# Second part of an attention and expert kernel: tiles at other addresses, a weight sum made by an adding load, operands stored in one piece

## The chip, the cores and the metric

The kernel runs on one core of a Trainium2 chip, in fp32. The metric is the device time of one execution in microseconds. The time of a version is the median of its runs.

## The reference

Four sequences of 1024 tokens with 1024 features are normalised. A linear attention with a running sum gives `s`. A feed-forward network with eight experts that share one pair of weights, where each expert takes at most 256 tokens, gives `g`. The result is `x + s * g`.

```python
q = jnp.einsum('bld,ed->ble', x, Wq) + bq          # x is the normalised input
k = jnp.einsum('bld,ed->ble', x, Wk) + bk
v = jnp.einsum('bld,ed->ble', x, Wv) + bv
phi_q, phi_k = jax.nn.elu(q) + 1.0, jax.nn.elu(k) + 1.0
kv_sum = jnp.cumsum(phi_k * v, axis=1)
context = (phi_q * kv_sum).reshape(B, L, D) * SCALE
s = jnp.einsum('bld,ed->ble', context, Wo) + bo
...
h = jax.nn.gelu(buf @ w1.T + b1, approximate=False) @ w2.T + b2   # F = 4096
gathered = jnp.where(keep[:, None], h[...], 0.0) * probs_flat[:, None]
out = jnp.zeros_like(x).at[token_idx].add(gathered)
...
return x + s * jax.nn.silu(out)
```

Only tokens that an expert keeps have a `g` that is not zero. So at most 2048 tokens need the network, the queries and the output product.

## The kernel before

**First part (to about 453 us).** It normalises the tokens, makes keys and values with their running sum for the first 2304 tokens, stores these sums in DRAM (`kvs`) and picks the 2048 tokens. Its tiles lie in pools that are closed at its end. The second part's pools take the same addresses, and a tile of the second part waits until the tile that lay there is done with.

**Second part.** The chosen tokens are worked on in two passes (`p`) of 1024. A pass has five stages of 14 products: four pairs `hidden` and `ffn_out`, one for each quarter of the 4096 hidden features, and then the pair `queries` and `result`. Each pair member multiplies two matrices of 1024 x 1024 with Strassen's scheme: each matrix is cut into quarters, and 7 products of quarters or of their sums take the place of 8. A product is 48 matmuls: each fp32 operand is split into a high part in fp32r (`cast`, on ScalarE) and a remainder (`low`, on VectorE), and three of the four combinations are multiplied. There are 140 products, numbered by a step `n`; `n0` is the step before a member's first product.

The work around the products is written out by hand. `on(n, phase, f)` hangs a piece on a step. At each step the program emits the matmuls and then the pieces of ten phases:

```python
PHASES = ("load", "pre", "cast0", "evac", "low0", "add", "cast1", "low1", "post", "raw")
```

The instructions of TensorE, VectorE, ScalarE and SP (SyncE, which issues loads and stores) keep this order. [...] 

The pieces that matter here:

- `left_weights` loads the four quarters of a left weight matrix (`left_quarter`, SP, 1 MB each, L766) into five tiles `raw` of 8 KB a partition that `right_weights` uses in turn (L1055), and makes the sums on VectorE (`sub` at L930, `plus` at L933). At step `n0 + 1`, phase `pre`, a sum and a difference are made that product `n0 + 2` needs.
- `fetched` loads the tokens' operands of the next product (1 MB for each half, L976) from DRAM tensors `xtd`, in which the seven operands of a pass lie in split form. Those of the first pass are stored from the tiles that the products use (`keep`, L1100). Those of the second are made by `xprep_items` during steps 14 to 20 and 28 to 34: gather four times (L647), transpose (L240), add, split (L166, L167), store from a tile `o` (L679).
- `Unit` is a tile with one half of a product's operand; `a` and `b` have three each, used in turn, two in the pool `fu`, the third in `fp`.
- `queries` gathers the key sums of its tokens (`fetch`, 16 gathers `gk` on POOL for each quarter), transposes them (`turn`), and multiplies them into the evacuated quarter (`then`, L1228 and L1233).
- `result` adds its four quarters to the output by scatters that add (`done`, L1292, on POOL).
- `small` gives tiles of 4 KB a partition from a pool `sp` of nine. It serves gathers, transposed sums, exponentials, `o`, and also the rows of the biases `b2` and `bo`. `ps` is one of two PSUM tiles of four banks; a product group begins when one of them is evacuated.

Of the kernel before, what the change touches and what calls it, by code (L numbers as in the profile page):

```python
# [18 lines left out]
P = 128  # L19
# [27 lines left out]
def tile_first_tokens(  # L47
# [44 lines left out]
    xtd = [dp.tile([7 * 2 * P, 4 * BT], F32, name=f"xtd_{p}") for p in range(NP)]  # L92
# [562 lines left out]
    def xprep_items(p, buf):  # L655
# [3 lines left out]
        def item(j):  # L659
# [13 lines left out]
            def out_of(i, src):  # L673
                o = buf(f"o{p}_{j}_{i}")
                oh = o.bitcast(F32R).rearrange("p (u h k t) -> h p u k t", u=2, h=2, k=2)
                split((oh[0], oh[1]), src.rearrange("p (u k t) -> p u k t", u=2, k=2))
                dst = xtd[p].rearrange("(i u p) (s t) -> i u p s t", i=7, u=2, s=4)[i - 1]
                for u, ou in enumerate(o.rearrange("p (u s t) -> u p s t", u=2, s=4)):
                    nc.gpsimd.dma_start(dst[u, :, :, j * P : (j + 1) * P], ou)  # L679

            def plain():
                out_of(1, v[0, 0])
                out_of(2, v[1, 0])

            def sums():
                t = buf(f"t{p}_{j}")
# [5 lines left out]
            def sums2():  # L692
                nc.vector.tensor_tensor(v[0, 1], v[1, 1], v[0, 1], ALU.subtract)
                nc.vector.tensor_tensor(v[1, 0], v[1, 0], v["t2"], ALU.subtract)
                out_of(7, v[0, 1])
                out_of(5, v["t1"])

            def rest():
                out_of(4, v[1, 0])
                out_of(3, v[1, 1])  # L700

            return fetch, turn, plain, sums, sums2, rest
# [61 lines left out]
    def left_quarter(dst, src, i, j):  # L764

        nc.sync.dma_start(  # L766
            dst.rearrange("p m (k f) -> p m k f", k=4),
            src[4 * i : 4 * i + 4, :, 4 * j : 4 * j + 4].rearrange("m p k f -> p m k f"),
        )
# [9 lines left out]
    class Unit:  # L779


        def __init__(self, side, i):

            pool = later["fu" if (i + 1) % 3 < 2 else "fp"]
            self.t = pool.tile(
                [P, 2, 2 * BT], F32R, tag=f"{side}{(i + 1) % 3}", name=name(side)
            )
# [96 lines left out]
    store_sums(queue=nc.gpsimd)  # L884
# [11 lines left out]
    sp = ctx.enter_context(tc.tile_pool(name="sp", bufs=9, reuse_waits="tile"))  # L896

    sp.tile([P, 2 * P], F32, tag="room", bufs=1, name="room")
    fp = ctx.enter_context(tc.tile_pool(name="fp", bufs=1, reuse_waits="tile"))
    later["fp"] = fp  # L900
    fps = ctx.enter_context(tc.tile_pool(name="fps", bufs=2, space=PSUM, reuse_waits="tile"))
# [15 lines left out]
    raw += [quarter(f"raw_{i}") for i in range(2, 5)]  # L917
# [6 lines left out]
    yq[0] = quarter("y0")  # L924
# [56 lines left out]
    def tokens(p, i):  # L981
        return xtd[p].rearrange("(i u p) f -> i u p f", i=7, u=2)[i - 1]
# [43 lines left out]
    def left_weights(n0, src, view=None):  # L1026

        q = dict(zip(((0, 0), (1, 0), (1, 1), "t", (0, 1)), raw))
        raw[:] = (q[k] for k in ((0, 0), "t", (1, 0), (1, 1), (0, 1)))
# [8 lines left out]
        on(max(n0 - 2, -1), "raw", lambda: load((1, 1)))  # L1038
        on(n0 - 1, "raw", lambda: load((0, 1)))

        on(n0, "add", lambda: sub(q["t"], q[0, 0], q[1, 0]))
        on(n0 + 1, "pre", lambda: plus(q[1, 0], q[1, 0], q[1, 1]))
        on(n0 + 1, "pre", lambda: sub(q[0, 0], q[1, 0], q[0, 0]))
        on(n0 + 3, "add", lambda: sub(q[0, 1], q[0, 1], q[0, 0]))
        for k, key in enumerate(((0, 0), (0, 0), (0, 1), "t", (1, 0), (1, 1), (0, 1))):
# [113 lines left out]
    def ffn_out(n0, h, s, y):  # L1159
# [18 lines left out]
        if s == 0:  # L1178

            def row():  # L1180
                y["b"] = small("b2")
# [9 lines left out]
    def queries(n0, p):  # L1191
# [48 lines left out]
        for k, d, key in (  # L1240
            (-14, 2, (0, 0)), (-12, 2, (1, 1)), (-6, 3, (1, 0)), (1, 2, (0, 1))
# [23 lines left out]
    def result(n0, h, y, p):  # L1265
# [4 lines left out]
        def row():  # L1270
            c["b"] = small("bo")
# [62 lines left out]
    for p in range(NP):  # L1334
        y = dict(yq)
        if p + 1 < NP:
            prep = xprep_items(p + 1, small)
            for j, (s, at) in enumerate(
                ((s, at) for s in (1, 2) for at in ((0, 2, 2, 2, 3, 4), (2, 4, 4, 5, 5, 6)))
            ):  # L1340
# [97 lines left out]
```

## Time and profile before

| | |
|---|---|
| median of 3 runs | 2067.14 us (2067.07 to 2069.58) |
| the profiled execution | 2073.87 us, span 2072.1 us |
| TensorE busy | 1978.2 us, 95% |
| VectorE busy | 1508.6 us, 73% |
| ScalarE busy | 756.9 us, 37% |
| POOL busy | 421.7 us, 20% |
| moved by DMA | 360.32 MB, 174 GB/s on average |
| idle time of TensorE before the second part's matmuls | 52.6 us |

A row of a timeline gives start, duration, engine, line, operation, what is written from what, shape and count; in brackets stands the idle time of the engine before it and what ended it. Like instructions that follow each other closely are merged. `PE` is TensorE, `DVE` VectorE, `ACT` ScalarE; a `q` behind a name means the engine's queue. In a row of windows each engine's busy time and count of instructions follow the stretch, then TensorE's clock and the DMA engines' share and GB/s.

### The profile page before, as it was taken

What the parts mean: (1) busy time and instruction counts of PE and PEld (TensorE: products, weight loads), DVE (VectorE), ACT (ScalarE), POOL (GpSimd) and SP (SyncE); (2) the same over time, 40 slices, a digit from 0 to 9 for tenths busy, and PEclk for the clock granted to TensorE, in tenths of its full rate; (3) what the DMA queues carried; (4) which work ended last, traced back from release to release, by engine and by line L of the source; (5) the groups of instructions that cost most, each with busy time, mean ns of one, the idle gap of its engine ahead of it and who ended that gap; (6) DMA issues with size and microseconds to landing.
All of it is one profiled execution on the core that took longest, in us unless ns stands there. A gap on an engine that the chain in (4) does not pass through costs nothing.

```text
span 2072.1 us, 22267 instructions
## 1 busy us (share of the span) xinstructions
PE 1978.2 (95%) x8840; PEld 1631.3 (79%) x8840; DVE 1508.6 (73%) x1376; ACT 756.9 (37%) x874; POOL 421.7 (20%) x387
## 2 busy tenths in 40 slices
PE   7999999989999999999999889899999999999875
PEld 6877878877887887888887677788888888888764
DVE  7868876577876876975887785585685685787884
ACT  2323332225533433532423453342432432343451
POOL 1001104652003502843020068001000001120013
PEclk9999999999999999999999989999999999999988
DMA  8867849638248448447146148515515416426314
GB/s 305 242 195 234 264 124 193 190 80 347 74 147 327 156 146 328 146 163 279 54 162 256 51 103 257 209 62 197 199 61 219 167 61 248 158 82 253 133 21 63
DMA packets 114290, 360.32 MB, mean 174 GB/s; under 512 B 13216, under 2 KB 37792, under 8 KB 96032
## 3 DMA queue, kind: packets, MB, share of 16 engines
q1 hardware_dynamic: 77504, 299.98, 41.1%
q0 software_dynamic: 18240, 42.56, 7.7%
q10 hardware_dynamic: 18432, 16.26, 3.5%
q8 instruction: 72, 1.18, 0.2%
q14 instruction: 42, 0.34, 0.0%
HBM read 292.66 MB, written 73.42 MB: 177 GB/s over the span
## 4 chain that ended last, share of the span: by engine, by line
PE 79%; DVE 6%; issue 6%; POOL 3%; DMA 3%; ACT 2%; ACTq 0%; SPq 0%; DVEq 0%; POOLq 0%
PE ps L1005 61%; PE pk L160 3%; PE pk L161 3%; PE pk L162 3%; PE pv L162 3%; PE pv L160 3%; PE pv L161 3%; POOL gk L647 2%; DMA b<-xtd 2%; POOL out L1292 1%; PE pl L325 1%; DVE hid L1228 1%; DVE hid L933 1%; DVE hid L1233 1%; DMA kvs<-kr 0%
## 5 line engine op out<-in xcount | busy, mean ns | idle before, releaser
L1005 PE MATMUL ps<-b,a 128*128 128x512 f32 x6720 | 1544.5, 392 | 52.6 <-DVE y L933 19.2
L1005 PEld LDWEIGHTS ps<-b,a 128*128 128x128 f32 x6720 | 1271.3, 189 | 325.5 <-issue 26.1
L793 ACT CAST a<-raw 128x1024 fp32r<-128x1024 f32 x140 | 147.2, 1052 | 456.8 <-PE ps L1005 366.4
L647 POOL DMA_INDIRECT gk<-kvs,eighth x128 | 174.0, 1360 | 668.4 <-DVE kv L240 504.8
L796 DVE TENSOR_TENSOR a<-raw,a 128x1024 fp32r<-128x1024 f32 x140 | 170.6, 1221 | 182.7 <-ACT a L793 178.1
L793 ACT CAST a<-hid 128x1024 fp32r<-128x1024 f32 x120 | 126.1, 1051 | 368.9 <-PE ps L1005 261.1
L796 DVE TENSOR_TENSOR a<-hid,a 128x1024 fp32r<-128x1024 f32 x120 | 146.4, 1220 | 64.8 <-ACT a L793 64.6
L796 DVE TENSOR_TENSOR b<-raw,b 128x1024 fp32r<-128x1024 f32 x140 | 170.8, 1220 | 1.6 <-ACT b L793 1.6
L933 DVE TENSOR_TENSOR hid<-ps,hid 128x2048 f32<-128x2048 f32 x52 | 119.0, 2288 | 63.7 <-PE ps L1005 48.7
L930 DVE TENSOR_TENSOR raw<-raw,raw 128x2048 f32<-128x2048 f32 x70 | 160.3, 2290 | 1.1
L793 ACT CAST b<-raw 128x1024 fp32r<-128x1024 f32 x140 | 146.7, 1048 | 1.8 <-DMA xtd<-b 1.8
L933 DVE TENSOR_TENSOR work<-ps,work 128x2048 f32<-128x2048 f32 x40 | 91.5, 2288 | 48.8 <-PE ps L1005 48.8
L160 PE MATMUL pk<-xt,ws_w 128*128 128x512 f32 (+1 forms) x264 | 103.1, 391 | 2.6 <-issue 1.4
L161 PE MATMUL pk<-xt,ws_w 128*128 128x512 f32 (+1 forms) x264 | 102.9, 390 | 2.5 <-issue 1.3
L162 PE MATMUL pv<-xt,ws_w 128*128 128x512 f32 (+1 forms) x264 | 101.3, 384 | 1.3 <-DVE ws_w L167 1.2
L162 PE MATMUL pk<-xt,ws_w 128*128 128x512 f32 (+1 forms) x264 | 102.6, 388 | 0.0
L160 PE MATMUL pv<-xt,ws_w 128*128 128x512 f32 (+1 forms) x264 | 101.6, 385 | 0.0
L161 PE MATMUL pv<-xt,ws_w 128*128 128x512 f32 (+1 forms) x264 | 101.2, 383 | 0.0
L679 POOL DMA_DIRECT2D xtd<-o x56 | 41.4, 876 | 277.9 <-DVE o L167 277.2
L166 ACT CAST ws_w<-wr_w 128x1024 fp32r<-128x1024 f32 x64 | 66.1, 1048 | 82.7 <-issue 39.7
L167 DVE TENSOR_TENSOR ws_w<-wr_w,ws_w 128x1024 fp32r<-128x1024 f32 x64 | 77.8, 1215 | 14.7 <-ACT ws_w L166 11.2
L361 ACT ACTIVATE kb<-pk,bs 128x512 f32<-128x512 f32 (+1 forms) x40 | 25.8, 646 | 134.1 <-PE pk L162 97.2
(183 smaller groups left out, 1653.3 us busy)
## 6 DMA issues: line engine op xcount, KB each, us to landing
b<-xtd SPq DMA_DIRECT2D x126, 1024.0 KB
raw<-in_w SPq DMA_DIRECT2D x64, 1024.0 KB
wr_w<-in_wk SPq DMA_DIRECT2D x32, 512.0 KB
wr_w<-in_wv SPq DMA_DIRECT2D x32, 512.0 KB
xtd<-b SPq DMA_DIRECT2D x14, 1024.0 KB
xtd<-o POOLq DMA_DIRECT2D x56, 256.0 KB
kvs<-kr ACTq DMA_DIRECT2D x32, 256.0 KB
raw<-in_wq SPq DMA_DIRECT2D x8, 1024.0 KB
```

The lines of the kernel that those rows point to most:

```text
L160: nc.tensor.matmul(ps, ws[:, 0, k], mv[:, 0, k, c0:c1], start=k == 0, stop=False)
L161: nc.tensor.matmul(ps, ws[:, 0, k], mv[:, 1, k, c0:c1], start=False, stop=False)
L162: nc.tensor.matmul(ps, ws[:, 1, k], mv[:, 0, k, c0:c1], start=False, stop=k == DC - 1)
L166: nc.scalar.copy(dst[0], src)
L167: nc.vector.tensor_tensor(dst[1], src, dst[0].bitcast(F32), ALU.subtract)
L647: nc.gpsimd.indirect_dma_start(out=dst, out_offset=None, in_=src, in_offset=bass.IndirectOffsetOnAxis(ap=idx, axis=0),)
L679: nc.gpsimd.dma_start(dst[u, :, :, j * P : (j + 1) * P], ou)
L793: nc.scalar.copy(self.parts[0], src)
L796: nc.vector.tensor_tensor(self.parts[1], self.src, self.parts[0].bitcast(F32), ALU.subtract)
L930: nc.vector.tensor_tensor(dst, a, b, ALU.subtract)
L933: nc.vector.tensor_tensor(dst, a, b, ALU.add)
L1005: nc.tensor.matmul(ps[:, m], a(h, k, m), b(l, k), start=s["first"] and u == 0 and k == 0 and i == 0, stop=u == 1 and k == 1 and i == 2, sk ...
```

## The change

1. The tensor `xtd` gets one row of 4096 numbers for each operand and partition, so that an operand piece `o` is stored by one DMA of 512 KB instead of two of 256 KB. The stages of `xprep_items` are cut finer and spread over the steps in another way.
2. One sum of two weight quarters, `q["t"]`, is made by loading one quarter and then loading the second onto it with an adding DMA on POOL's queue, at step `n0 - 1`. The second of these quarters is loaded once more by itself, at step `n0`. The sum on VectorE goes, and the difference is made in place.
3. The pool `fp` is laid out first, in the order room, row, the third units of `a` and `b`, `y0`, `raw_4`, `raw_2`, `raw_3`; `sp` comes behind it, with eight tiles instead of nine. The bias rows and the sums `t` of `xprep_items` use the tile `row`.
4. The last stores of `kvs` are issued from ScalarE's queue instead of POOL's.
5. The last `turn` of `queries` comes three steps after its `fetch` instead of two.

```diff
--- before.py
+++ after.py
@@ -89,7 +89,7 @@
     lst = dp.tile([nt, 2], I32, name="lst")


-    xtd = [dp.tile([7 * 2 * P, 4 * BT], F32, name=f"xtd_{p}") for p in range(NP)]
+    xtd = [dp.tile([7 * P, 2 * 4 * BT], F32, name=f"xtd_{p}") for p in range(NP)]


     ident = kp.tile([P, P], F32, name="ident")
@@ -674,32 +674,33 @@
                 o = buf(f"o{p}_{j}_{i}")
                 oh = o.bitcast(F32R).rearrange("p (u h k t) -> h p u k t", u=2, h=2, k=2)
                 split((oh[0], oh[1]), src.rearrange("p (u k t) -> p u k t", u=2, k=2))
-                dst = xtd[p].rearrange("(i u p) (s t) -> i u p s t", i=7, u=2, s=4)[i - 1]
-                for u, ou in enumerate(o.rearrange("p (u s t) -> u p s t", u=2, s=4)):
-                    nc.gpsimd.dma_start(dst[u, :, :, j * P : (j + 1) * P], ou)
-
-            def plain():
-                out_of(1, v[0, 0])
-                out_of(2, v[1, 0])
+                dst = xtd[p].rearrange("(i p) (s t) -> i p s t", i=7, s=8)[i - 1]
+                nc.gpsimd.dma_start(
+                    dst[:, :, j * P : (j + 1) * P], o.rearrange("p (s t) -> p s t", s=8)
+                )
+
+            def plain(i):
+                out_of(i, v[i - 1, 0])

             def sums():
-                t = buf(f"t{p}_{j}")
+                t = one(f"t{p}_{j}")
                 v["t1"], v["t2"] = t[:, :BT], t[:, BT:]
                 nc.vector.tensor_tensor(v["t1"], v[0, 1], v[0, 0], ALU.subtract)
                 nc.vector.tensor_tensor(v["t2"], v[1, 1], v["t1"], ALU.subtract)
                 out_of(6, v["t2"])

-            def sums2():
+            def sum7():
                 nc.vector.tensor_tensor(v[0, 1], v[1, 1], v[0, 1], ALU.subtract)
+                out_of(7, v[0, 1])
+
+            def sum4():
                 nc.vector.tensor_tensor(v[1, 0], v[1, 0], v["t2"], ALU.subtract)
-                out_of(7, v[0, 1])
-                out_of(5, v["t1"])
-
-            def rest():
                 out_of(4, v[1, 0])
-                out_of(3, v[1, 1])
-
-            return fetch, turn, plain, sums, sums2, rest
+
+            return (
+                fetch, turn, lambda: plain(1), lambda: plain(2), sums, sum7,
+                lambda: out_of(5, v["t1"]), sum4, lambda: out_of(3, v[1, 1]),
+            )

         return [item(j) for j in range(NJ)]

@@ -761,11 +762,12 @@
         nc.vector.tensor_tensor(work[:, 2], work[:, 3], work[:, 2], ALU.subtract)
         nc.vector.tensor_tensor(ht, work[:, 2], work[:, 0], ALU.add)

-    def left_quarter(dst, src, i, j):
-
-        nc.sync.dma_start(
+    def left_quarter(dst, src, i, j, queue=nc.sync, **how):
+
+        queue.dma_start(
             dst.rearrange("p m (k f) -> p m k f", k=4),
             src[4 * i : 4 * i + 4, :, 4 * j : 4 * j + 4].rearrange("m p k f -> p m k f"),
+            **how,
         )


@@ -781,10 +783,12 @@

         def __init__(self, side, i):

-            pool = later["fu" if (i + 1) % 3 < 2 else "fp"]
-            self.t = pool.tile(
-                [P, 2, 2 * BT], F32R, tag=f"{side}{(i + 1) % 3}", name=name(side)
-            )
+            place = (i + 1) % 3
+            tag = f"{side}{place}"
+            self.t = later.pop(tag, None)
+            if self.t is None:
+                pool = later["fu" if place < 2 else "fp"]
+                self.t = pool.tile([P, 2, 2 * BT], F32R, tag=tag, name=name(side))

         def cast(self, src):
             self.src = src
@@ -881,7 +885,7 @@
                 xt = nxt
         finish()

-    store_sums(queue=nc.gpsimd)
+    store_sums()
     first.close()


@@ -893,11 +897,16 @@

-    sp = ctx.enter_context(tc.tile_pool(name="sp", bufs=9, reuse_waits="tile"))
-
-    sp.tile([P, 2 * P], F32, tag="room", bufs=1, name="room")
+
+
     fp = ctx.enter_context(tc.tile_pool(name="fp", bufs=1, reuse_waits="tile"))
     later["fp"] = fp
+    fp.tile([P, 2 * P], F32, name="room")
+    later["row"] = fp.tile([P, D], F32, tag="row", name="row")
+    later.update(
+        (f"{side}2", fp.tile([P, 2, 2 * BT], F32R, tag=f"{side}2", name=f"{side}2"))
+        for side in "ab"
+    )
     fps = ctx.enter_context(tc.tile_pool(name="fps", bufs=2, space=PSUM, reuse_waits="tile"))
     bq1, nbq = (cp.tile([P, DC], F32, name=n) for n in ("bq1", "nbq"))
     nc.gpsimd.tensor_scalar(bq1, bq, 1.0, None, ALU.add)
@@ -914,14 +923,21 @@

-    raw += [quarter(f"raw_{i}") for i in range(2, 5)]
+    y0 = quarter("y0")
+    last_raw = quarter("raw_4")
+    raw += [quarter(f"raw_{i}") for i in range(2, 4)] + [last_raw]
+    sp = ctx.enter_context(tc.tile_pool(name="sp", bufs=8, reuse_waits="tile"))
     hid = big.tile([P, 4, NK, BT], F32, tag="xt", name="hid")

     hq = {(i, j): hid[:, 2 * i + j] for i in range(2) for j in range(2)}
     hq["t"] = ht

     yq = {(i, j): work[:, 2 * i + j] for i in range(2) for j in range(2)}
-    yq[0] = quarter("y0")
+    yq[0] = y0
+
+    def one(n):
+        t = later.pop("row", None)
+        return fp.tile([P, D], F32, tag="row", name=name(n)) if t is None else t

     def small(n):
         return sp.tile([P, D], F32, tag="s4", name=name(n))
@@ -979,7 +995,7 @@
         plan_at(n)["bview"] = all_chunks

     def tokens(p, i):
-        return xtd[p].rearrange("(i u p) f -> i u p f", i=7, u=2)[i - 1]
+        return xtd[p].rearrange("(i p) (u f) -> i u p f", i=7, u=2)[i - 1]

     def flat(x):
         return x.t.bitcast(F32).rearrange("p h f -> p (h f)")
@@ -1025,8 +1041,8 @@

     def left_weights(n0, src, view=None):

-        q = dict(zip(((0, 0), (1, 0), (1, 1), "t", (0, 1)), raw))
-        raw[:] = (q[k] for k in ((0, 0), "t", (1, 0), (1, 1), (0, 1)))
+        q = dict(zip(((0, 0), (1, 0), "t", (1, 1), (0, 1)), raw))
+        raw[:] = (q[k] for k in ((0, 0), (1, 0), "t", (1, 1), (0, 1)))

         def load(*keys):
             for key in keys:
@@ -1035,14 +1051,19 @@
         if n0:
             on(n0 - 4, "raw", lambda: load((0, 0)))
             on(n0 - 3, "raw", lambda: load((1, 0)))
-        on(max(n0 - 2, -1), "raw", lambda: load((1, 1)))
+
+        on(n0 - 2, "raw", lambda: left_quarter(q["t"], src, 1, 0))
+        on(
+            n0 - 1, "load",
+            lambda: left_quarter(q["t"], src, 1, 1, nc.gpsimd, accum_op=ALU.add),
+        )
         on(n0 - 1, "raw", lambda: load((0, 1)))
-
-        on(n0, "add", lambda: sub(q["t"], q[0, 0], q[1, 0]))
-        on(n0 + 1, "pre", lambda: plus(q[1, 0], q[1, 0], q[1, 1]))
-        on(n0 + 1, "pre", lambda: sub(q[0, 0], q[1, 0], q[0, 0]))
+        on(n0, "raw", lambda: load((1, 1)))
+
+        on(n0, "add", lambda: sub(q[1, 0], q[0, 0], q[1, 0]))
+        on(n0 + 1, "pre", lambda: sub(q[0, 0], q["t"], q[0, 0]))
         on(n0 + 3, "add", lambda: sub(q[0, 1], q[0, 1], q[0, 0]))
-        for k, key in enumerate(((0, 0), (0, 0), (0, 1), "t", (1, 0), (1, 1), (0, 1))):
+        for k, key in enumerate(((0, 0), (0, 0), (0, 1), (1, 0), "t", (1, 1), (0, 1))):
             built(n0 + 1 + k, "a", lambda key=key: q[key], by_blocks, of_blocks)

     def right_weights(n0, src, ahead=0):
@@ -1178,7 +1199,7 @@
         if s == 0:

             def row():
-                y["b"] = small("b2")
+                y["b"] = one("b2")
                 nc.gpsimd.dma_start(y["b"], rows[0:1, :].broadcast_to([P, D]))

             on(n0, "load", row)
@@ -1238,7 +1259,7 @@
         h = features(n0, p, wq, act, then)

         for k, d, key in (
-            (-14, 2, (0, 0)), (-12, 2, (1, 1)), (-6, 3, (1, 0)), (1, 2, (0, 1))
+            (-14, 2, (0, 0)), (-12, 2, (1, 1)), (-6, 3, (1, 0)), (1, 3, (0, 1))
         ):
             on(n0 + k, "load", lambda key=key: fetch(*key))
             on(n0 + k + d, "post", lambda key=key: turn(*key))
@@ -1268,7 +1289,7 @@
         c = {}

         def row():
-            c["b"] = small("bo")
+            c["b"] = one("bo")
             nc.gpsimd.dma_start(c["b"], rows[1:2, :].broadcast_to([P, D]))

         on(n0, "load", row)
@@ -1335,9 +1356,8 @@
         y = dict(yq)
         if p + 1 < NP:
             prep = xprep_items(p + 1, small)
-            for j, (s, at) in enumerate(
-                ((s, at) for s in (1, 2) for at in ((0, 2, 2, 2, 3, 4), (2, 4, 4, 5, 5, 6)))
-            ):
+            ats = ((0, 2, 2, 2, 2, 3, 3, 3, 4), (2, 4, 4, 5, 4, 5, 5, 6, 6))
+            for j, (s, at) in enumerate((s, at) for s in (1, 2) for at in ats):
                 for k, (d, f) in enumerate(zip(at, prep[j])):
                     on(n0 + 14 * s + d, "post" if k else "load", f)
         for s in range(NQ):
```

## The prediction

> **What bounds the kernel now.** I read the page first (TensorE is busy for 95% of the 2072.1 us span), then TensorE's own timeline over the second part. There its 140 products of 48 matmuls run almost back to back: 13 undisturbed products take 141.70 us, 10.9 us each. So only TensorE's gaps count.
>
> ```profile
> 468.05 0.73 PE L1005 MATMUL ps<-b,a 128*128 128x512 f32 x1 [4.22 <-ACT b L793]
> 469.50 187.99 PE L1005 MATMUL ps<-b,a 128*128 128x512 f32 x815 [0.72 <-DVE b L796]
> 659.38 11.14 PE L1005 MATMUL ps<-b,a 128*128 128x512 f32 x48 [1.88 <-DMA b<-xtd]
> 671.33 141.70 PE L1005 MATMUL ps<-b,a 128*128 128x512 f32 x624 [0.81 <-DMA b<-xtd]
> 815.53 317.43 PE L1005 MATMUL ps<-b,a 128*128 128x512 f32 x1392 [2.49 <-DMA b<-xtd]
> ...
> 1287.82 0.70 PE L1005 MATMUL ps<-b,a 128*128 128x512 f32 x2 [0.94 <-issue]
> 1288.91 10.72 PE L1005 MATMUL ps<-b,a 128*128 128x512 f32 x46 [0.38 <-DVE a L796]
> 1306.13 622.83 PE L1005 MATMUL ps<-b,a 128*128 128x512 f32 x2736 [6.50 <-DMA b<-xtd]
> ...
> 1966.57 0.73 PE L1005 MATMUL ps<-b,a 128*128 128x512 f32 x1 [3.74 <-DVE hid L933]
> 1968.75 13.13 PE L1005 MATMUL ps<-b,a 128*128 128x512 f32 x47 [1.44 <-DVE b L796]
> 1991.63 0.76 PE L1005 MATMUL ps<-b,a 128*128 128x512 f32 x1 [9.76 <-DVE y L933]
> ```
>
> See five places: the entry (468), the two stretches in which the next 1024 tokens are prepared (659 to 815), the change from the first tokens to the second (1288 to 1306), and each pass's switch from queries to result (1966 and 1991; in the first pass 1170 and 1195). ScalarE's row behind the entry names a landing:
>
> ```profile
> 466.01 1.04 ACT L793 CAST a<-raw 128x1024 fp32r<-128x1024 f32 x1 [16.29 <-DMA kvs<-kr]
> ```
>
> VectorE's rows before the second switch are a row without a hole:
>
> ```profile
> 1904.02 2.64 DVE L240 STREAM_TRANSPOSE kv<-gk 128x512 f32<-128x512 f32 x4
> ...
> 1926.87 4.62 DVE L930 TENSOR_TENSOR raw<-raw,raw 128x2048 f32<-128x2048 f32 x2
> 1931.40 2.28 DVE L933 TENSOR_TENSOR hid<-ps,hid 128x2048 f32<-128x2048 f32 x1
> ```
>
> POOL's queue at the change of tokens has 32 gathers ahead of the scatters:
>
> ```profile
> 1208.96 1.95 POOL L1292 DMA_INDIRECT out<-c,half x1 [0.30 <-issue]
> 1211.22 1.02 POOL L647 DMA_INDIRECT gk<-kvs,eighth x1 [0.30 <-issue]
> ...
> 1269.93 0.94 POOL L647 DMA_INDIRECT gk<-kvs,eighth x1 [0.30 <-issue]
> 1271.17 1.62 POOL L1292 DMA_INDIRECT out<-hid,half x1 [0.30 <-issue]
> ```
>
> The windows of the preparing products show the DMA engines full (the two numbers at the end: share, GB/s):
>
> ```profile
> 646.50:657.40 10.90, 10.90 (x49) 8.78 (x47) 6.88 (x9) 6.12 (x10) 4.97 (x8) 1.00 1.02 399
> ```
>
> The sum is made against this execution, which took 2073.87 us (1.8 around its span) and stands 6.7 above the median of 2067.14; I carry the difference over to the median.
>
> **Part 1, order of addresses: -7.** The first cast of product 2 waits until 466 because its tile lies where the last key rows lay, until their store has landed. After the change that tile and its partner come early in their pool, over tiles that TensorE reads last, free at 452.8. What is late next is VectorE: its difference at 456.76 is as before and ends at 459.05, then one difference (2.29) instead of a sum and a difference, to 461.3. ScalarE now also issues the last four key stores, after the four that it issues from 455.12 to 458.5 (3.38 us); the same again ends at 461.9. Two casts (1.04 each) and the second remainder (1.22) give product 2 at about 465.2. TensorE is free at 463.84, so 1.4 idle are left. The stores of the tokens' operands on SP, behind a load that sat until 465.44, start some 8 us sooner too. They still take 9.6 us to land (465.90 to 475.5 before), so the second half's cast is due at about 467, and its remainder is ready before 470.6, when it is needed. Product 3 then starts at 476.1 instead of 483.3. Bounds: nothing, and the whole 8.8 lost between 452.77 and 483.3 (30.5 less two products).
>
> [...] The row at 469.50 holds 815 matmuls in 188.0 us, 2.9 more than at the pace of the row at 671.33, and that row follows a gap of 0.81 with no loss. [...] By the idle rows alone the entry gives 4.2 + 0.7 - 1.4 = 3.5; with the slow matmuls 7. I take 7: the excess is in the rows. A long gap below gets 2.1 on top for the same reason (the 383 matmuls from 1197.81, after the gap of 9.42, take 89.08 us, 2.1 over pace).
>
> **Part 2, tokens' operands stored whole, over more products: -0.5.** 56 stores of 256 KB become 28 of 512 KB. POOL's issue time (41.4 us in all) does not matter: nobody on the path waits for it there. Bytes and pieces of 512 B stay the same. Stores per product go from 3, 2, 4, 3, 2 to 3, 3, 3, 3, 2, in a stretch where the engines are full for three products (1.02 at 399 to 407 GB/s). The peak falls by one store of 512 KB, 1.3 us at 400 GB/s, but the product with two weight loads gets one more. The stretches cost 5.2 idle and about 1.6 slow. I take -0.5, between -4 and +4. VectorE's and ScalarE's work is only moved within products that have room (6.88 and 6.12 of 10.9 busy in the row above).
>
> **Part 3, one row tile apart, eight small tiles, the turn one product later: +5.3.** The four transposes for the last quarter of the queries (2.64) move from step n0+3, where VectorE then waits for ScalarE anyway (1.66 before the row at 1908, 4.36 before 1913.9), to step n0+4. There they stand in front of 1922.28, in the hole-free row. Evacuation (1931.4), ScalarE's exponentials (1933.7 to 1938.9), remainder, products with the gathered rows, the next evacuation: each starts when the one before ends, up to the evacuations that TensorE waits for at 1966.57 and 1991.63. Both move by 2.64, once per pass. Least: 0 if slack opens; most: 2.64 each. I take all, twice.
>
> **Part 4, the adding load.** Per set of left weights it removes one sum of 2.29 on VectorE, ten in all, mostly where VectorE has room; I count nothing but the entry's. It adds one load of 1 MB on SP and one adding load of 1 MB on POOL, 20 MB over 2 ms; the late load of the fourth quarter is needed five products on. The adding load waits for the plain load ahead of it. Behind it on POOL stand gathers and scatters; nobody is short of these except at the change of tokens.
>
> In nine of the ten places POOL is idle or waiting for something later when it is due. At the change of tokens it is not. The plain load waits for a difference that ends at 1228.5. The adding load is ready at about 1234, and is needed when VectorE reaches the sum it replaces, at 1252.4. The 32 gathers are then in their middle. [...] Its flight has no row. The nearest are the adding scatters: one of 256 KB landed 8.45 after its issue, four together 14.1 after the first. I take 10. [...]
>
> So it lands at 1281.2. Difference 2.29, evacuation and product in front of the remainder 4.6, remainder 1.2: product 72 starts at 1289.3 instead of 1265. That is 24.3 idle and 2.1 slow. It swallows the stop of before (0.94 + 0.38 + 6.50 idle, about 2.6 slow), whose scatters land meanwhile. Net +16.0; with 8.45 and 14.1 it is +14.5 and +20.1; the gathers falling elsewhere makes it 0, or -10.
>
> **Sum.** -7 - 0.5 + 5.3 + 16.0 = +13.8 on 2067.1: 2080.9.
>
> **Rivals.**
> [...]
> - *Faster: the gathers no longer stand before the scatters.* Fewer small tiles might hold them back until their turn. Then the stop of before goes as well: -12.6, 2054.5. Against it: e1 and c11 hold four tiles, and four of eight are left for 32 gathers.
> - *The change doesn't do what it says at the entry.* If the adding load or ScalarE's stores hold product 2 to 468, the gain is 0: with the rest in time +4.8, 2072.
>
> **How the numbers follow.** Late adding load 0.55 (2070 to 2092: flight, entry and stretches at their bounds); in time 0.27; no gathers ahead 0.13; no gain at the entry 0.05. The time is the likeliest's, 2080.9. The range goes down to 2058, which takes in most of the second case and leaves out the third, and up to 2092. A measurement tells about 0.2%, 4.1 us, from no change. Faster by more: 0.01 + 0.11 + 0.12 = 0.24; within: 0.01 + 0.09 + 0.03 = 0.13; slower: 0.53 + 0.07 + 0.01 + 0.02 = 0.63.
>
> **What would show it.** Right: product 2 within 2 us of product 1's end; a VectorE wait of some 25 us on the adding load at the change of tokens, with TensorE idle behind it; the gaps at the switches 2.6 longer. Wrong: the adding load ahead of the gathers, no idle there, or VectorE's switch no later than before. Stops of over 5 us at a store of tokens' operands would refute part 2.

## The result, and the profile after

The change takes 2090.07 us (median of 4 executions, 2086.06 to 2092.91) against 2067.11 (2066.93 to 2069.58): a ratio of 1.0107, 95% interval 1.0086 to 1.0128, so 23 us slower. In a second comparison, on another chip, it was 1.0106 (1.0089 to 1.0122). The profiled execution took 2092.11 us with a span of 2090.3.

The loss is read from TensorE's own timeline. The second part consists of 140 products, and an undisturbed one takes 10.88 us from its start to the start of the next. What a product takes beyond 10.893 us is counted as lost (so 47 products without any stop show -0.6). These are TensorE's rows after the change (start, duration, engine, line, operation, count, and in brackets the idle time before and what ended it):

```profile
447.30 11.07 PE L1021 MATMUL ps<-b,a 128*128 128x512 f32 x48
476.55 0.79 PE L1021 MATMUL ps<-b,a 128*128 128x512 f32 x1 [18.18 <-ACT b L797]
478.04 187.35 PE L1021 MATMUL ps<-b,a 128*128 128x512 f32 x815 [0.70 <-DVE b L800]
667.50 154.12 PE L1021 MATMUL ps<-b,a 128*128 128x512 f32 x672 [2.10 <-DMA b<-xtd]
...
1209.52 67.21 PE L1021 MATMUL ps<-b,a 128*128 128x512 f32 x287 [1.41 <-DVE b L800]
1291.42 1.19 PE L1021 MATMUL ps<-b,a 128*128 128x512 f32 x2 [14.70 <-ACT a L797]
1294.84 654.52 PE L1021 MATMUL ps<-b,a 128*128 128x512 f32 x2878 [2.22 <-DVE a L800]
...
1989.35 0.77 PE L1021 MATMUL ps<-b,a 128*128 128x512 f32 x1 [4.03 <-DVE hid L949]
1991.53 12.66 PE L1021 MATMUL ps<-b,a 128*128 128x512 f32 x47 [1.41 <-DVE b L800]
2014.40 0.77 PE L1021 MATMUL ps<-b,a 128*128 128x512 f32 x1 [10.21 <-DVE y L949]
```

The gap at the entry is now 18.18 us, where it was 4.22 before; product 2 follows product 1 with a long hole. The gap at the change of tokens is new (14.70 and 2.22), and the three small stops that were there have gone. The table sums what was lost by place, in the two profiled executions; the prediction's terms stand beside it.

| place (products) | before | after | difference | predicted |
|---|---|---|---|---|
| entry (1 to 3) | 8.7 | 22.1 | +13.4 | -7 |
| preparation (4 to 48) | 7.0 | 7.8 | +0.8 | -0.5 |
| first switch (49 to 69) | 23.1 | 26.0 | +2.9 | +2.6 |
| change of tokens (70 to 78) | 10.9 | 19.7 | +8.8 | +16.0 |
| second switch (126 to 139) | 22.9 | 26.4 | +3.5 | +2.6 |
| last product's end to the end of the span | 22.2 | 16.5 | -5.7 | 0 |

The differences add up to +23.7, and the medians differ by 23.0. The first part ended at 452.8 in the profiled execution of before and at 447.3 after; in two other profiled executions of kernels that keep the first part of before (below) it ended at 444.4 and 446.3, so I do not count these 5.5 us for the change.

At the entry, VectorE's row names the adding load as what it waits for (L946 is the difference `sub`):

```profile
472.12 2.29 DVE L946 TENSOR_TENSOR raw<-raw,raw 128x2048 f32<-128x2048 f32 x1 [20.84 <-DMA raw<-in_w]
```

And POOL's timeline shows what stood in front of that load. L603 to L620 fetch and turn the lists of chosen tokens, L1203 is the bias row, L767 the adding load:

```profile
438.61 0.78 POOL L615 DMA_DIRECT2D it<-lst  x1
441.72 1.17 POOL L620 TENSOR_SCALAR half<-it 128x4 int32<-128x4 int32 x2 [2.32 <-DMA it<-lst]
451.57 0.56 POOL L1203 DMA_DIRECT2D row<-in_rows  x1 [8.68 <-DVE kr L417]
452.13 1.38 POOL L767 DMA_DIRECT2D raw<-in_w  x1
```

In this execution POOL is idle for 8.68 us with the bias row at its head, because the row's tile lies over key rows that VectorE still writes. The row goes out at 451.57, the adding load behind it starts at 452.13, and VectorE has it at 472.1, after 20 us. At that time eight stores of key rows leave on ScalarE's queue. Their issue alone takes 12.47 us (second and third row below), against 3.38 for the four that ScalarE issued before (first row):

```profile
455.12 3.38 ACTq L424 DMA_DIRECT2D kvs<-kr  x4
449.67 12.47 ACTq L424 DMA_DIRECT2D kvs<-kr  x8
474.50 1.04 ACT L797 CAST a<-raw 128x1024 fp32r<-128x1024 f32 x1 [30.23 <-DVE raw L946]
```

At the change of tokens, POOL's timeline has the picture that the prediction drew, the adding load behind the last of 32 gathers and ahead of the scatters:

```profile
1208.37 2.03 POOL L647 DMA_INDIRECT gk<-kvs,eighth  x1 [0.30 <-issue]
...
1274.07 0.94 POOL L647 DMA_INDIRECT gk<-kvs,eighth  x1 [0.30 <-issue]
1275.01 1.46 POOL L767 DMA_DIRECT2D raw<-in_w  x1
1276.77 1.64 POOL L1313 DMA_INDIRECT out<-hid,half  x1 [0.30 <-issue]
```

VectorE waits for it until 1286.83:

```profile
1262.88 1.22 DVE L800 TENSOR_TENSOR a<-raw,a 128x1024 fp32r<-128x1024 f32 x1
1286.83 2.29 DVE L946 TENSOR_TENSOR raw<-raw,raw 128x2048 f32<-128x2048 f32 x1 [22.73 <-DMA raw<-in_w]
1289.04 2.28 DVE L949 TENSOR_TENSOR y<-ps,y 128x2048 f32<-128x2048 f32 x1
```

At the second switch, two rows of before and three of after show VectorE's transposes (L240) in the row without a hole:

```profile
1921.15 1.22 DVE L796 TENSOR_TENSOR a<-raw,a 128x1024 fp32r<-128x1024 f32 x1
1922.28 2.28 DVE L933 TENSOR_TENSOR hid<-ps,hid 128x2048 f32<-128x2048 f32 x1
...
1941.55 1.22 DVE L800 TENSOR_TENSOR a<-raw,a 128x1024 fp32r<-128x1024 f32 x1
1942.69 2.48 DVE L240 STREAM_TRANSPOSE kv<-gk 128x512 f32<-128x512 f32 x4
1945.09 2.25 DVE L949 TENSOR_TENSOR hid<-ps,hid 128x2048 f32<-128x2048 f32 x1
```

From the remainder (L800) to the evacuation (L949) is 3.54 us now. It was 1.13 before, so the evacuation comes 2.4 later.

### The profile page after: what moved, and what is told of

Same layout as the page of the kernel before. It is cut to its first block, busy times and chain, and to the rows that moved or that the text cites. A ratio compares the mean times of both kernels' runs of the same rounds, so it can differ in the third digit from the quotient of the medians.

```text
span 2090.3 us, 22273 instructions
## 1 busy us (share of the span) xinstructions
PE 1978.1 (95%) x8840; PEld 1631.0 (78%) x8840; DVE 1487.2 (71%) x1366; ACT 756.1 (36%) x874; POOL 410.2 (20%) x365
## 4 chain that ended last, share of the span: by engine, by line
PE 76%; DVE 9%; DMA 6%; ACT 3%; POOL 3%; issue 3%; ACTq 0%; SPq 0%; DVEq 0%; POOLq 0%
PE ps L1021 61%; PE pk L160 2%; PE pk L161 2%; PE pk L162 2%; PE pv L162 2%; PE pv L160 2%; PE pv L161 2%; POOL gk L647 2%; DMA raw<-in_w 2%; DMA b<-xtd 1%; DVE hid L1249 1%; DVE a L800 1%; DVE raw L946 1%; DVE hid L949 1%; PE pl L325 1%
## 5 line engine op out<-in xcount | busy, mean ns | idle before, releaser
L1021 PE MATMUL ps<-b,a 128*128 128x512 f32 x6720 | 1547.2, 392 | 79.3 <-DVE y L949 19.8
L800 DVE TENSOR_TENSOR a<-raw,a 128x1024 fp32r<-128x1024 f32 x140 | 170.2, 1221 | 179.8 <-ACT a L797 179.8
L647 POOL DMA_INDIRECT gk<-kvs,eighth x128 | 167.9, 1312 | 266.5 <-DVE kv L240 228.7
L946 DVE TENSOR_TENSOR raw<-raw,raw 128x2048 f32<-128x2048 f32 x70 | 160.2, 2288 | 61.8 <-DMA raw<-in_w 43.6
L800 DVE TENSOR_TENSOR a<-hid,a 128x1024 fp32r<-128x1024 f32 x120 | 146.4, 1220 | 64.0 <-ACT a L797 63.8
L800 DVE TENSOR_TENSOR b<-raw,b 128x1024 fp32r<-128x1024 f32 x140 | 170.6, 1218 | 1.7 <-ACT b L797 1.7
L949 DVE TENSOR_TENSOR hid<-ps,hid 128x2048 f32<-128x2048 f32 x52 | 118.9, 2287 | 54.4 <-PE ps L1021 54.4
L949 DVE TENSOR_TENSOR work<-ps,work 128x2048 f32<-128x2048 f32 x40 | 91.5, 2288 | 52.0 <-PE ps L1021 52.0
L767 POOL DMA_DIRECT2D raw<-in_w x8 | 11.0, 1379 | 546.0 <-ACT a L797 445.1
L167 DVE TENSOR_TENSOR ws_w<-wr_w,ws_w 128x1024 fp32r<-128x1024 f32 x64 | 77.8, 1215 | 14.6 <-ACT ws_w L166 14.6
```

What stands on the lines that cost most here:

```text
L167: nc.vector.tensor_tensor(dst[1], src, dst[0].bitcast(F32), ALU.subtract)
L647: nc.gpsimd.indirect_dma_start(out=dst, out_offset=None, in_=src, in_offset=bass.IndirectOffsetOnAxis(ap=idx, axis=0),)
L800: nc.vector.tensor_tensor(self.parts[1], self.src, self.parts[0].bitcast(F32), ALU.subtract)
L946: nc.vector.tensor_tensor(dst, a, b, ALU.subtract)
L949: nc.vector.tensor_tensor(dst, a, b, ALU.add)
L1021: nc.tensor.matmul(ps[:, m], a(h, k, m), b(l, k), start=s["first"] and u == 0 and k == 0 and i == 0, stop=u == 1 and k == 1 and i == 2, sk ...
```

## The experiments

My theory: the change loses its time in separate places, each with its own cause. The adding load is late at the entry by its place in POOL's queue, and at the change of tokens behind the gathers; the later turn costs at the switches. The rivals, tested place by place: the order of addresses and the stores that ScalarE now issues, the bytes of the adding loads, the whole stores. Every ratio below is against the kernel before on the same chip. "Lost" is TensorE's loss as in the table above, in the profiled execution. Among the chips, one ran the first part 13 us slower than the others, for the kernel before too (2081.13 us there); ratios and places can be compared, absolute times cannot.

**The change again.** The kernel is that of the change.

> The change once more, beside the kernels that undo parts of it, since chips differ by more than the parts do. Theory: 1.008 to 1.013 of the kernel before also here; TensorE loses 22 us at the entry, 20 at the change of tokens and 26 at each switch. Rival (the long flight of the adding load at the entry was one execution's bad luck): the entry loses 10 or less.

Measured: 2090.08 us, 1.0106 (1.0089 to 1.0122). Lost: entry 22.2, change of tokens 19.7, switches 26.4 and 26.4. The loss at the entry is no accident of one execution: all places repeat within 0.4 us, but for preparation at 0.8. What held the adding load up did not repeat, though:

```profile
451.22 0.34 POOL L620 TENSOR_SCALAR half<-it 128x4 int32<-128x4 int32 x2 [1.76 <-DMA it<-lst]
451.79 0.56 POOL L1203 DMA_DIRECT2D row<-in_rows  x1 [0.22 <-issue]
452.34 1.38 POOL L767 DMA_DIRECT2D raw<-in_w  x1
```

Here the token lists are done only at 451.6, not at 442.9, and the bias row waits 0.22 us instead of 8.68. The load starts at nearly the same time all the same, and VectorE has it 19.5 us later. So either of the two things in front of it is late enough.

**No adding load.** In `left_weights` the quarters (1,0) and (1,1) are loaded by themselves and VectorE sums them:

```
-        on(n0 - 2, "raw", lambda: left_quarter(q["t"], src, 1, 0))
-        on(n0 - 1, "load",
-            lambda: left_quarter(q["t"], src, 1, 1, nc.gpsimd, accum_op=ALU.add))
...
-        on(n0, "raw", lambda: load((1, 1)))
+        on(max(n0 - 2, -1), "raw", lambda: load((1, 1)))
-        on(n0, "add", lambda: sub(q[1, 0], q[0, 0], q[1, 0]))
-        on(n0 + 1, "pre", lambda: sub(q[0, 0], q["t"], q[0, 0]))
+        on(n0, "add", lambda: sub(q["t"], q[0, 0], q[1, 0]))
+        on(n0 + 1, "pre", lambda: plus(q[1, 0], q[1, 0], q[1, 1]))
+        on(n0 + 1, "pre", lambda: sub(q[0, 0], q[1, 0], q[0, 0]))
...
```

> The change with the adding load taken back alone (each weight quarter loaded by itself, the sum made on VectorE, as before); the other order of addresses, the whole stores and the later turn stay. Theory (the entry and the change of tokens wait for the adding load): TensorE's time lost at the entry falls from 22.1 us to about 1.5, at the change of tokens from 19.8 to the 10.9 of the kernel before, the switches keep 26.2 and 26.5; about 2060.6 us, 29.5 below the change and some 6 below the kernel before. Rival (the key stores that ScalarE now issues, or the address order itself, hold the entry): the entry keeps 20 us or more, only the 8.9 of the change of tokens come back, about 2081.

Measured: 1.0022 (1.0004 to 1.004), so 0.84% or 17.4 us less than the change's 1.0106. The edit takes away the adding load and, with it, the second load of quarter (1,1) by SP. Lost: entry 5.1, change of tokens 11.1, switches 25.1 and 25.5. Both places fall as the theory says and the rival falls: the order of addresses does not hold the entry at 20. But the sum was missed by 12 us: the kernel stays 0.2% above the kernel before, not 6 us under it. Of these, 3.6 are the entry, which ends at 5.1 and not at 1.5, and 6.3 come back at the end of the span (22.8 from the last product's end, against 16.5). The rest I cannot place; the two kernels ran on different chips. What is left at the entry shows in ScalarE's row:

```profile
463.51 7.54 ACTq L424 DMA_DIRECT2D kvs<-kr  x8
472.18 1.04 ACT L797 CAST a<-raw 128x1024 fp32r<-128x1024 f32 x1 [14.07 <-DMA kvs<-kr]
```

Eight key stores take 7.54 us to issue, and VectorE's three sums end at 472.1 (the last starts at 469.80 and takes 2.29). The two are through at nearly the same time.

**Adding load in nine places, not at the entry.** `left_weights` calls the version above where `n0 == 0`:

```
+        if n0 == 0:
+            return left_weights_first(n0, src)
```

> The adding load in nine of its ten places; only the first set of left weights, at the entry, is loaded quarter by quarter and summed on VectorE. Theory (each place has its own price): the entry falls to about 1.5 us lost, the change of tokens keeps 19.8; about 2069.5 us. Rival (entry held by something else): 2090, VectorE's wait of 20.8 at the entry goes but TensorE still starts its second product 20 us late. Second rival (the adding loads cost little but by their bytes on full DMA queues all through): it stays within 3 us of the change.

Measured: 1.0036 (1.0025 to 1.0047), 14.5 us less than the change, where 20.6 was expected; 2.7 of the missing 6 stand at the end of the span. Lost: entry 3.6, change of tokens 18.5, switches 25.6 and 27.4. Each place keeps its own price; both rivals fall. With the entry at 3.6 against 8.7, the order of addresses, together with ScalarE's stores, gains some 5 us there.

**Bias row on SP.** One word is changed:

```
-                nc.gpsimd.dma_start(y["b"], rows[0:1, :].broadcast_to([P, D]))
+                nc.sync.dma_start(y["b"], rows[0:1, :].broadcast_to([P, D]))
```

> The change with the broadcast of the bias row issued by SP in its place instead of by POOL, where it stands in front of the adding load at the entry and waits until 451.57 us. Theory (place in POOL's queue is the cause): the plain load was issued at 439.15, so the adding load starts by about 446 and lands near 452, the second product follows the first within 2 us; 20 us less, about 2070. Rival (the adding load waits for the plain load's end or for its tile anyway): it still starts near 451.6 and lands at 471 in the burst of stores; within 2 us of 2090. Second rival (the flight is long by what flies beside it): starts at 446, but lands after 460: 8 to 12 us less, about 2080.

Measured: 1.005 (1.0029 to 1.0072), 11.6 us less than the change. Lost: entry 7.6. POOL's row:

```profile
450.54 1.36 POOL L767 DMA_DIRECT2D raw<-in_w  x1 [3.35 <-PE pk L162]
```

The first part ended at 461.3 here, so the load starts 10.8 us ahead of that end; in the change it started 4.8 behind it. VectorE did not wait for it at all, and the entry loses 14.6 us less. (The 439.15 of the expectation is quarter (0,1). The load onto which the adding load adds went out at 430.81 in the change and landed at 436.12, so it held nothing up.) But in this execution the first part was 14 us later and POOL's lists only 4.3, which helps the load; hence the next run.

**Bias row on SP, once more.** The same kernel on another chip.

> The kernel with the bias row on SP once more: its first run had a first part that ended at 461.5 us, the change's at 447, and so 14 us more for POOL's work ahead of the adding load. Theory (the adding load starts when POOL is through with the token lists and with what stands in front): with a first part of 447 it starts at about 443 where the lists end as they did in the change (442.9), the entry loses 5 to 9 instead of 22; about 14 us less than the change. Rival (POOL's lists end later in other executions: 450.4 with the gathers between, 461.2 with the turn at two): it starts after 450 and the entry loses 17 or more although no row is in front.

Measured: 1.0095 (1.0079 to 1.011). Lost: entry 14.5, between both expectations. The adding load started at 444.86, right behind the lists, and VectorE had it at 453.81, 8.9 us later. Yet product 2 started at 467.88, and ScalarE's row tells why:

```profile
447.69 18.05 ACTq L424 DMA_DIRECT2D kvs<-kr  x8
465.84 1.04 ACT L797 CAST a<-raw 128x1024 fp32r<-128x1024 f32 x1 [23.55 <-DMA kvs<-kr]
```

Eight key stores held ScalarE for 18.05 us, and the casts of product 2 stand behind them. So there are two late things at the entry, one behind the other: the adding load, and when that is in time, ScalarE's own queue. In the change the second, through at 462.1, was hidden by the first, through at 474.4.

**Gathers at their own steps.** POOL keeps gathers, bias rows and adding loads in the order of the program:

```
     def gather(dst, src, idx):
-        in_turn(
+        tc.keep_in_program_order(
```

with the same call around the bias row and the adding load.

> The change with the gathers, the bias rows and the adding loads held in the order of the program on POOL; so the 32 gathers of the second tokens' queries come behind the adding load and the scatters at the change of tokens, at their own steps 40 products later. Theory: the adding load at the change of tokens starts some 59 us sooner and lands in time, the scatters' stop is gone as well, 19.8 us lost become about 1.5; about 2072 us. Rival (gathers at their own step are late for their turns): VectorE waits for them before steps 114 and 116, 32 gathers at 1.85 are 59 us for two products' time; what is saved comes back there, 2085 to 2095. Second rival (the adding load's flight or the plain load in front is what is late): VectorE still waits 10 us or more; about 2082.

Measured: 1.0195 (1.0143 to 1.0247). At the change of tokens 4.9 are lost instead of 19.7, as the theory says, but 19.8 at products 45 and 46 and 22.5 at 115 and 116 are new. The first rival has the place right, not the mechanism. The transposes of gathered rows do not wait; TensorE and VectorE stop in small pieces with nothing named, while POOL issues 48 gathers in a row (912.5 to 978.8):

```profile
960.12 0.86 PE L1023 MATMUL ps<-b,a 128*128 128x512 f32 x3 [1.07 <-issue]
962.95 0.39 PE L1023 MATMUL ps<-b,a 128*128 128x512 f32 x1 [1.97 <-issue]
...
972.18 0.94 PE L1023 MATMUL ps<-b,a 128*128 128x512 f32 x3 [0.74 <-issue]
```

What "issue" stands for here stays open. One thing goes with it, as cause or as effect: the 16 KB packets on the queue that the page calls instruction come 35.8 and then 41.3 us apart (from 932.4 on), against 26.1 and 31.2 at that place in the change. To have the gathers at their own steps costs more than it saves.

**Gathers between.** The 32 gathers for the second tokens are emitted 24 products ahead of their place and kept in order on POOL, behind the last scatters. The adding load and the bias row are kept in order too (not shown here):

```
-            on(n0 + k, "load", lambda key=key: fetch(*key))
+            at = n0 + k - 24 if p and k < -10 else n0 + k
+            on(at, "load", lambda key=key: fetch(*key))
```

> The change with the 32 gathers of the second tokens' queries put between the last scatter and their turns, 24 products ahead of where the program has them, and POOL held in program order from there. Theory: the change of tokens falls from 19.8 us lost to 2 or less, and what holding them at their own steps cost (16.5 and 6.0 at products 115 and 116) does not come back; 18 us less than the change. Rival (the adding load comes late at the change of tokens by its plain load or its flight): 10 or more stay lost there. Second rival (gathers in the midst of the second tokens' products collide with the loads): losses of over 5 us at products 88 to 100.

Measured: 1.0063 (1.0046 to 1.008), 0.43% or 8.9 us less than the change; its profiled execution was the lowest of four (2073.87, median 2078.42). Lost at the change of tokens: 3.7 instead of 19.7, 16 less. Nothing comes back at the later products (-0.6 from 79 to 125, as in every kernel). The adding load now starts behind its plain load, and VectorE uses it without a wait:

```profile
1240.32 1.35 POOL L767 DMA_DIRECT2D raw<-in_w  x1 [23.39 <-DMA raw<-in_w]
1255.13 2.29 DVE L948 TENSOR_TENSOR raw<-raw,raw 128x2048 f32<-128x2048 f32 x1
```

What is left is two stops of 0.49 and 2.83 at loads of token operands. The entry kept 21.1, although the bias row now stands behind the adding load there: the lists on POOL ended at 450.5 in this execution, and the load started at 450.76. That is the rival expected of the bias row on SP once more, seen here.

**Turn after two products.** The second gathered tile of the fourth quarter lies in the row tile:

```
-            g = kvt["g", i, j] = [small("gk") for _ in range(2)]
+            g = kvt["g", i, j] = [
+                small("gk"), one("gk") if (i, j) == (0, 1) else small("gk")
+            ]
...
-            (-14, 2, (0, 0)), (-12, 2, (1, 1)), (-6, 3, (1, 0)), (1, 3, (0, 1))
+            (-14, 2, (0, 0)), (-12, 2, (1, 1)), (-6, 3, (1, 0)), (1, 2, (0, 1))
```

> The change with the turn of the fourth quarter back at two products after its gathers; the second of its two gathered tiles lies in the row tile, so that eight small tiles are enough. Theory (the turn's 2.64 us of transposes stand in VectorE's hole-free row): the two switches fall from 26.2 and 26.5 to the 23.3 and 22.9 of the kernel before, 6.5 us less than the change. Rival (the loss at the switches comes from the ten adding loads, the bytes or the other order): they keep 26. Second rival (the output row, which now waits for this tile, comes late): over 2 us lost at the products after the switch.

Measured: 1.0077 (1.006 to 1.0094), 6.0 us less than the change. Lost at the switches: 23.0 and 23.5, as before the change, and nothing new behind them. Entry (25.2) and change of tokens (19.6) keep theirs.

**Gathers between, alone on the kernel before.** The same shift and the bias row kept in order, in the kernel before.

> The kernel before with one mend alone: the 32 gathers of the second tokens' queries 24 products ahead of their place and behind the last scatters. Theory: the 10.9 us lost at the change of tokens fall to about 0, entry 8.5, preparation 7 and switches 46 stay; 10 to 11 us or 0.5% under the kernel before. Rival (scatters are late by their own time, or the gathers collide with loads): under 4 us.

Measured: 2057.35 against 2066.73 us, 0.9952 (0.9939 to 0.9966). The change of tokens loses nothing (-0.1 instead of 10.9); the other places stay within 1.5 us.

**Whole stores, alone on the kernel before.** `xtd`, `xprep_items` and `ats` are those of the change, the rest is the kernel before.

> The kernel before with the second part of the change alone: tokens' operands stored whole, spread over more products. Theory of the prediction: -0.5 us, between -4 and +4, all of it in the preparing products (7.0 lost). Rival (whole stores cost in the full stretch, as 10.8 lost with both mends suggest): 9 or more lost there, +2 to +4 us.

Measured: 0.9994 (0.9985 to 1.0003). Lost in the preparation: 7.8 against 7.0. That cannot be told from no change.

**No adding load, both mends.** The edits of three experiments together: no adding load, gathers between, turn after two products.

> No adding load, the turn at two products, the gathers between scatters and turns: the change's order of addresses and whole stores alone, with the two places mended. Theory (losses add up place by place): entry 4 to 5 lost instead of 8.5, change of tokens 1 instead of 10.9, switches 46.2 as before, preparation 8: about 59.5 lost against 71.8 of the kernel before, 12 us or 0.6% under it. Rival (the mends take from each other; gathers moved run into a load): no better than 0.2% under the kernel before.

Measured: 2055.86 against 2067.3 us, 0.9942 (0.9925 to 0.9958). Lost: entry 5.1, preparation 10.8, switches 22.9 and 23.1, change of tokens -0.1; 61.3 in all. The places add up, but for 3 us in the preparation.

**The same with stores in halves.** Additionally `xtd`, `xprep_items` and `ats` are those of the kernel before. Of the change are left the order of addresses with the small tiles, and ScalarE's stores.

> No adding load, both mends, and the tokens' operands stored in halves as before: of the change only the order of addresses is left. Theory (whole stores cost 0 to 4): preparation 7 lost instead of 10.8; 12 to 15 us under the kernel before, 0 to 4 under the version with whole stores. Rival (the 3.8 there were chance): equal to it within 1 us.

Measured: 2054.35 against 2066.73 us, 0.994 (0.9926 to 0.9953). Preparation: 9.2. The version with whole stores has 0.9942, so the rival holds: whole stores are worth nothing either way. TensorE's row from the first switch to the queries of the second tokens has no gap any more:

```profile
1188.54 720.24 PE L1022 MATMUL ps<-b,a 128*128 128x512 f32 x3167 [1.41 <-DVE b L801]
```

This is the best version, 12.4 us under the kernel before. Most of that is the gathers' place (9.4 us in the run with that alone), and the entry gives about 4 in the trace (4.8 lost against 9.2); the two medians lie 3.0 apart, and their intervals overlap.

## Why the prediction was right or wrong

The forecast was 2080.9 us and slower; it is 2090.1, near the upper end of the range. The direction and the steps at the switches, the stores and the change of tokens hold; the step at the entry had the wrong sign. That the number still came out inside is in part luck: the entry missed by 20.4 us, and 7.2 too much at the change of tokens and 5.7 at the end of the span made up for over half of it. Of the signs named for being right, "product 2 within 2 us of product 1's end" failed (18.18), while the wait on the adding load (22.73, "some 25") and the longer gaps at the switches came.

- **Part 1, the entry: wrong.** The sum said -7, it is +13.4. The step that failed is in part 4: "In nine of the ten places POOL is idle or waiting for something later when it is due." At the entry the token lists and the bias row stand ahead of the adding load. The profile of before already had the row's wait for key rows, at the head of POOL's queue:

```profile
457.01 0.57 POOL L1182 DMA_DIRECT2D b<-in_rows  x1 [10.41 <-DVE kr L417]
```

  The text asked what stands in front of the adding load at one place only. How late the load starts goes with what the entry loses, over the seven profiles that have it there:

| kernel | start of the adding load, against the first part's end | entry lost |
|---|---|---|
| bias row on SP | 10.8 before | 7.6 |
| gathers at their own steps | 5.7 before | 6.2 |
| bias row on SP, once more | 0.5 before | 14.5 |
| the change | 4.8 behind | 22.1 |
| the change again | 5.6 behind | 22.2 |
| gathers between | 7.5 behind | 21.1 |
| turn after two products | 16.6 behind | 25.2 |

  The second mis-sized term is ScalarE's issue of eight key stores: twice 3.38 was reckoned, it took 7.4 to 7.7 in the kernels without an adding load at the entry, and 9.6 to 18.5 with one. The order of addresses does what was said, in part: without an adding load the entry loses 3.6 to 5.1 instead of 8.7. So it gains about 4 to 5, not 7.
- **The slow matmuls after a gap: right.** At the change of tokens 16.9 us are idle and 19.7 are lost. The granted clock (the number behind the five engines) is in the windows of that place:

```profile
1265.70:1276.60 10.90, 10.90 (x49) 8.81 (x47) 0.00 (x0) 0.00 (x0) 8.63 (x9) 1.00 0.86 312
1276.60:1291.40 14.80, 0.12 (x1) 0.01 (x1) 4.54 (x3) 2.17 (x3) 12.50 (x8) 0.68 1.04 214
1291.40:1295.40 4.00, 1.75 (x3) 1.00 (x4) 4.00 (x3) 2.53 (x2) 2.48 (x2) 0.50 1.13 204
1295.40:1306.30 10.90, 10.90 (x42) 8.80 (x41) 2.88 (x3) 1.05 (x1) 5.88 (x4) 0.84 0.97 150
```

  It is 1.00 ahead of the gap of 14.70 us and 0.50 behind it. The 2.1 added for the slow matmuls measured 2.8.
- **Part 2, whole stores: right.** Predicted -0.5 between -4 and +4; alone it measured -0.06% with an interval that holds zero.
- **Part 3, the turn: right, a little small.** Predicted 2.64 for each switch, measured 2.9 and 3.5; taking it back alone gave 3.4 and 2.9 against the change on the same chip, and 6.0 us in all.
- **Part 4, the change of tokens: place right, size off.** No run shows what sets the order of POOL's queue, on which the start at 1271.2 rested. What the runs showed is the place: before, the first scatter of `hid` was issued at 1271.17, behind 32 gathers that took 59.65 us (from 1211.22 on); after, the adding load was issued at 1275.01, behind all 32 gathers and ahead of the scatters of `hid`, and the stop of before vanished. +16.0 was predicted, +8.8 measured. The term is the start of the row of gathers. Before, it began 15.6 us behind product 66's start (1211.22 against 1195.63), and the text kept that. After, it began 1.0 behind (1208.37 against 1207.34). As the four scatters of `c` now stand among the gathers, the adding load started 66.6 us later instead of 60.0. That makes it 7.9 us earlier than reckoned. The flight, taken as 10, was 11.7 (1275.01 to 1286.7). From the landing, product 72 took 4.7 and a stop of 2.2 where 8.1 was reckoned; the other differences are under 1 us. At the six quiet places of the change the adding loads land 8.4 to 8.8 us after their issue.
- **Not in the sum: the end of the span.** It is 5.7 us shorter after the change. It was 16.2 to 20.2 in all eight profiles of kernels with an adding load, 20.8 to 23.3 in the six without. The last scatter is issued 7.7 us behind TensorE's end in the eight and 8.2 to 8.3 in the six; nearly all the difference lies behind that issue. Why is open.
- **The rivals.** The adding load in time (0.27) and no gathers ahead (0.13) fell with POOL's timeline (1275.01, behind all 32). "No gain at the entry" named the right cause, the adding load or ScalarE's stores holding product 2, with a chance of 0.05 and a gain of 0 at the entry; the first held it, the second stood right behind, and it cost 13.4.

## What to carry to other kernels

A transfer that moves to another engine's queue has to be placed in that queue at every one of its places: what is at the head there, what that waits for (8.68 us for the bias row at the entry of the change), and what else lands at that time. A late thing can hide a second one of nearly the same lateness, so taking away the wait that the profile names may give back only a part (22.2 to 14.5 lost at the entry, with the bias row on SP). And work that stands early in a queue can be cheap for itself but not for what stands behind it: moving the 32 gathers from before the scatters to between scatters and use gave 9.4 us, alone on the kernel before.

## What the runs showed of the hardware

- A row of stores held the engine that issues them. Four key stores took ScalarE 3.4 to 3.5 us in the kernels with the old order of addresses; eight took 7.4 to 7.7 without an adding load at the entry, and 9.6 to 18.5 with one. ScalarE's next cast stands behind the last store (at 465.84 behind 465.74, with the bias row on SP once more). In the change the sixth and the eighth were issued 0.02 us after the second and the third had landed (454.77 and 457.58), and the eighth took 4.54 us to issue. What stretches the row is not shown; it is not the adding load alone: with the turn after two products the row took 13.34 us (447.94 to 461.28), and the adding load was issued behind it, at 462.12. In every kernel with the long row SP's extra load of quarter (1,1) and two 1 MB stores of operands fall into it; in those with the short one SP's stores lie before or behind it. No run takes these apart.
- In the change the adding load of 1 MB landed 8.4 to 8.8 us after its issue at the six quiet places, 11.7 at the change of tokens, 14.1 and 13.1 at the sets of weights ahead of the two switches, and 20.0 at the entry; the plain loads of 1 MB on SP landed 5.9 after their issue (median of its page).
- Rows of 48 gathers on POOL (at their own steps) went with 19.8 and 22.5 us lost by TensorE in small stops that name only "issue". No run here tells why.
- On one chip the first part took some 13 us longer, in all four kernels that were profiled there (it ended at 459.6 to 461.3, elsewhere at 443.3 to 452.8). The stops lie between 385 and 415 us, and ScalarE's and VectorE's rows mostly name "issue" or "remote". It moved the entry too, by the place of POOL's work against the end of the first part: with the bias row on SP the entry lost 7.6 there and 14.5 elsewhere.
